# Layers 0 and 3 by image, and a recurrence that starts with one group of its input gates

## Chip, core and metric

One Trainium2 chip, one of its cores. The time is device time of one execution in microseconds; "before" is the median of three runs. Five engines work beside each other, each with an instruction queue of its own that it works off in order: TensorE (PE; its weight loads are shown as PEld), VectorE (DVE), ScalarE (ACT), GpSimd (POOL) and SyncE (SP), which here issues DMAs. All arithmetic is in float32.

## What is computed

Four layers on x of shape (4, 256, 32, 32): 4 images, 256 channels, 1024 tokens an image. The change touches layers 0 and 3; layer 1 (a rank-one attention with batch norm) and layer 2 (attention and a mixture of eight experts) stay.

```python
# layer 0: state-space block, then a gate per channel and image
u   = layernorm(tokens(x)) * norm_g + norm_b
y   = ssm(conv(in_proj(u))) * silu(z)
y   = y * rsqrt(mean(y * y, -1) + EPS) * rms_w
out = einsum('bld,ed->ble', y, out_w)
pooled = mean over tokens of out
attn   = sigmoid(relu(pooled @ se1_w.T + se1_b) @ se2_w.T + se2_b)
x   = x + out * attn
...
# layer 3: linear attention, then a recurrent cell over the tokens
f     = layernorm(t)
query = f @ W_qk[0] + b_qk[0];  key = f @ W_qk[1] + b_qk[1]
lam   = einsum('bnd,bne->bde', softmax(key, axis=1), f @ W_v + b_v)
bn    = batchnorm(lam) * gamma + beta          # over images and columns
t     = t + einsum('bnd,bde->bne', query, bn)
xi, xg, xo = (layernorm(t) @ U_k + b_k for k in 'ico')
for each of the 1024 tokens (all 4 images at once):
    i = sigmoid(xi_t + h @ V_i); g = tanh(xg_t + h @ V_c); o = sigmoid(xo_t + h @ V_o)
    c = h * c + i * g;  h = o * tanh(c)
t     = t + all h
```

The forget gate of the cell is computed in the reference but not used.

## The kernel before

The phases run one after another: set-up, layers 0 to 3. Instructions are written in source order; a scheduler in the framework then chooses their order on each engine by dependencies and estimated times, except where `_in_order` (L157) chains the instructions of a stretch of source on TensorE, VectorE and ScalarE so that each follows the one written before it. Tiles come from pools with a number of buffers; a tile waits until the buffer's last user is done, and a pool that opens on memory of a closed one waits for that one's users.

**Layer 0.** `_layer0` normalises and projects image by image and convolves. `_scan` (L376) goes over 8 chunks of 128 tokens, inside over the 4 images, 32 rounds: transposes and products on TensorE, an exp on ScalarE (L409), products with decays on VectorE and POOL, and at the end of a round the gated result in `zs` (L436). Then `_out_and_se` (L439) works over all images at once: 32 Squares on ScalarE with an accumulator (L449) give sums of squares per token; Sqrt and a reciprocal give rstd; then for each of 8 blocks of 512 tokens the rows are scaled (L459, VectorE), transposed (L463), evacuated with rms_w (L464), multiplied by out_w (L470), and evacuated by ScalarE with an accumulator that gives the sum over tokens (L473). After the last block come the mean, the two small products with Relu and Sigmoid (L478 to L491), and x is updated (L493). Layer 1's first products (L535) read x of all images.

**Layer 3, attention.** `_layer3_attention` (L1247) runs over images. Per image, two blocks of 512 tokens load two expert results each by SP's queue (L1282); POOL adds the two (L1285), VectorE adds them to x (L1287) and takes statistics (L1291, L1292). `_rsqrt` (L971) makes rstd for 8 columns by an integer start and four Newton steps of three VectorE operations. ScalarE normalises rows (L1302), TensorE turns them (L1268), VectorE copies them into `u` (L1273). Then key (L1318), its maximum, exp, transposed key times rows (L1343 to L1347), times W_v (L1357) give `lam` for the image; x is turned into `x_l` (ScalarE, L1271). After the images, `_batchnorm` on `lam` (L621 to L627, with a Sqrt), two passes for scale and shift (L1377, L1378), and the query weights are multiplied in once: `lam_q` (L1384) and `add_col` (L1394), so that later one product with `u` gives query times lam.

**Layer 3, recurrence.** `_layer3_lstm` (L1401) makes a few constants (L1429 to L1443). Tokens are in 8 groups of 128 steps. `ahead(n)` is a generator of parts for group n: `attended(n)` (attention output for these tokens, 16 parts of TensorE work and their adds, L1464 and L1458), then `input_gates(n)`: means (L1501), centring (L1487), squares, variance (L1511), Newton steps as "small" parts of one VectorE operation each, spread and p_r (L1545), and 64 parts for the gates, four for each of 16 sub-groups of eight steps (L1560, evacuated at L1571 into `xg`). Group 0's parts are run off before the first step. Each step then does: h times V (L1616, 48 products in three banks, TensorE), three transposes (L1645, VectorE), tanh and two sigmoids (L1646, ScalarE), the inputs of the next step from `xg` (L1607, TensorE), a scan for the cell (L1652), tanh (L1659), h (L1661) and the product for the next cell (L1663). One part of the next group's generator follows in each step; before the last step of a group all that are left are run off. `_in_order` fixes the order of all steps. POOL adds h to finished groups (L1585) and SP stores them.

Of the kernel before, what the change touches and what calls it, by code (L numbers as in the profile page):

```python
# [18 lines left out]
P = 128  # L19
# [47 lines left out]
NW = {"w_l0": 260 + 512 + 256 + 64, "w_l2": 768 + 8, "w_l3": 768, "w_u": 768, "w_v": 768}  # L67
# [91 lines left out]
def _in_order(s, start):  # L159


    engines = mybir.EngineType
    before = {}
    for i in s.nc.cur_bb.bb.instructions[start:]:
        if i.engine not in (engines.PE, engines.DVE, engines.Activation):
            continue
# [52 lines left out]
def _layer0(s):  # L219
# [6 lines left out]
    with ctx0 as ctx:  # L226
# [59 lines left out]
        _scan(s, xbc, zs, dt, decay, total, tail)  # L286
        _out_and_se(s, zs, w_out, w_se1, se2)
# [88 lines left out]
def _scan(s, xbc, zs, dt, decay, total, tail):  # L376
# [4 lines left out]
    with ExitStack() as ctx:  # L381
# [4 lines left out]
        for c in range(TPI):  # L386
            t = slice(off + c * P, off + (c + 1) * P)
            for b in range(B):
# [47 lines left out]
                nc.vector.tensor_mul(zs[:, n, :], zs[:, n, :], y.rearrange("p h d -> p (h d)"))  # L436


def _out_and_se(s, y, w_out, w_se1, se2):  # L439

    nc, tc = s.nc, s.tc
    with ExitStack() as ctx:
        keep = ctx.enter_context(tc.tile_pool(name="out_keep", bufs=1))
        pool = ctx.enter_context(tc.tile_pool(name="out", bufs=2))
        ps = ctx.enter_context(tc.tile_pool(name="out_ps", bufs=2, space=PSUM))
        ss = keep.tile([P, NT], F32, name="ss")
        for n in range(NT):
            sq = pool.tile([P, D], F32, name="sq")
            nc.scalar.activation(sq, y[:, n, :], AF.Square, accum_out=ss[:, n : n + 1])  # L449
        rstd = keep.tile([P, NT], F32, name="rstd")  # L450
        nc.scalar.activation(rstd, ss, AF.Sqrt, bias=s.eps, scale=1.0 / D)
        nc.vector.reciprocal(rstd, rstd)

        o = keep.tile([P, C, T], F32, name="o")
        part = keep.tile([P, C, NBLK], F32, name="part")
        for i in range(NBLK):
            yT = pool.tile([P, C, W], F32, name="yT")
            for n in range(i * TPB, (i + 1) * TPB):
                nc.vector.tensor_scalar_mul(y[:, n, :], y[:, n, :], rstd[:, n : n + 1])  # L459
            for k in range(C):  # L460
                pt = ps.tile([P, TPB, P], F32, name="pt")
                for j in range(TPB):
                    nc.tensor.transpose(pt[:, j, :], y[:, i * TPB + j, bass.ts(k, P)], s.ident)  # L463
                nc.vector.tensor_scalar_mul(  # L464
                    yT[:, k, :], pt.rearrange("p j q -> p (j q)"), s.col["rms_w"][:, k : k + 1]
                )
# [768 lines left out]
def _layer3(s):  # L1235
    with ExitStack() as ctx:
# [7 lines left out]
        _layer3_lstm(s, x, u, lam, add_col)  # L1244


def _layer3_attention(s, x, u, lam_q, add_col):  # L1247

# [513 lines left out]
```

## Time and profile before

| | us |
|---|---|
| median of three runs (3514.23 to 3514.61) | 3514.43 |
| profiled execution | 3514.67 |
| its span, first to last instruction | 3512.7 |
| TensorE busy | 3227.6 (92%) |
| VectorE busy | 2016.5 (57%) |
| ScalarE busy | 1245.0 (35%) |
| GpSimd busy | 416.3 (12%) |
| mean granted TensorE clock | 0.969 of full speed |

In the span, layer 0 ends and layer 1 begins near 359, the experts of layer 2 end near 1386, layer 3's first products with u start near 1426, step 1 of the recurrence at 1583, and the last h is there at 3506. A line of the timeline gives start and length in us, engine, line of the source, operation, output<-inputs and, in brackets, how long the engine sat idle before it and what ended that. A line of the windows gives the window and its length, then for PE, PEld, DVE, ACT and POOL the busy time and the number of instructions, then the granted clock of TensorE, the DMA engines' share and GB/s. "x16" counts instructions; a float32 product shows as two records. `x_l`, `u_l`, `w_l` are the names x_l3, u_l3 and w_l0, w_l2 or w_l3 with their numbers left out.

### The profile page before, as it was taken

The page shows a single profiled execution, that of the slowest core. Times are in us where ns is not written, and L with a number is a line of the kernel's source. Part 1 is how long each engine was busy: PE and PEld are TensorE (multiplying, and loading weights), DVE is VectorE, ACT ScalarE, POOL GpSimd, SP SyncE. Part 2 cuts the span into 40 slices and gives each one's busy share as a digit, 9 for nine tenths or more (in the row PEclk, how much of TensorE's full clock was granted, in tenths as well). Part 3 has the DMA queues.
Part 4 walks back from the last instruction along what each step waited for, and adds up shares of the span by engine and source line. Part 5 has one row for each costly group of instructions (what it writes and reads, how often), then busy time and mean ns, then how long its engine had stood idle before and what let it go on. Part 6 is the DMA issues. An engine that isn't in the chain of part 4 may idle for free.

```text
span 3512.7 us, 146893 instructions
## 1 busy us (share of the span) xinstructions
PE 3227.6 (92%) x65412; PEld 2536.4 (72%) x65412; DVE 2016.5 (57%) x8382; ACT 1245.0 (35%) x5047; POOL 416.3 (12%) x498
## 2 busy tenths in 40 slices
PE   7786899998999997789999999999999999999888
PEld 4464344447788886468888888888888888888776
DVE  5795534452211111747777776777777777767666
ACT  4623222223222222413334344343343343433333
POOL 0182001122433332100000000000000000000000
PEclk9898899999999999899999999999999999999999
DMA  1290001115556554100000000000000000000000
GB/s 67 80 303 5 9 0 37 37 50 197 195 189 219 208 190 165 60 2 4 4 11 4 5 10 4 4 10 4 6 9 5 10 4 5 10 4 5 10 4 10
DMA packets 79355, 189.31 MB, mean 54 GB/s; under 512 B 6592, under 2 KB 64256, under 8 KB 73728
## 3 DMA queue, kind: packets, MB, share of 16 engines
q0 software_dynamic: 16176, 116.06, 9.0%
q1 hardware_dynamic: 60624, 59.12, 5.7%
q8 instruction: 511, 8.37, 1.0%
q10 hardware_dynamic: 1920, 4.74, 0.4%
q14 instruction: 124, 1.02, 0.1%
HBM read 118.88 MB, written 61.02 MB: 51 GB/s over the span
## 4 chain that ended last, share of the span: by engine, by line
PE 41%; DVE 9%; ACT 4%; issue 2%; ACTq 0%; DVEq 0%
PE p_c L1616 11%; DVE turned L1645 7%; PE p_c L1607 7%; PE p_i L1607 4%; PE p_o L1607 4%; PE p_i L1616 4%; PE p_o L1616 4%; PE beside L1560 4%; ACT a_o L1646 2%; DVE x L1661 2%; ACT th L1659 2%; PE beside L1464 1%; PE beside L1501 0%; PE var L1511 0%; PE p_q L1384 0%
## 5 line engine op out<-in xcount | busy, mean ns | idle before, releaser
L1646 ACT ACTIVATE add<-turned 128x8 f32<-128x8 f32 x1024 | 214.3, 209 | 1027.5 <-DVE turned L1645 1027.5
L1616 PE MATMUL p_c<-w_v,x 128*4 128x64 f32 x16368 | 416.0, 219 | 72.8 <-DVE x L1661 71.0
L1607 PE MATMUL p_c<-xg,shift 128*128 128x64 f32 x2048 | 445.7, 299 | 0.0
L1616 PE MATMUL p_o<-w_v,x 128*4 128x64 f32 x16368 | 416.6, 219 | 0.1
L1616 PE MATMUL p_i<-w_v,x 128*4 128x64 f32 x16368 | 416.5, 219 | 0.0
L1607 PE MATMUL p_i<-xg,shift 128*128 128x64 f32 x2048 | 406.8, 280 | 0.0
L1645 DVE STREAM_TRANSPOSE turned<-p_c 128x64 f32<-128x64 f32 x1024 | 255.9, 250 | 257.1 <-PE p_c L1616 226.7
L1607 PE MATMUL p_o<-xg,shift 128*128 128x64 f32 x2048 | 396.0, 275 | 0.0
L1607 PEld LDWEIGHTS p_c<-xg,shift 128*128 128x128 f32 x2048 | 304.7, 188 | 117.6 <-issue 0.3
L1616 PEld LDWEIGHTS p_c<-w_v,x 128*4 128x4 f32 x16368 | 227.2, 85 | 196.3 <-DVE x L1661 121.2
L1661 DVE TENSOR_TENSOR x<-a_o,th 128x8 f32<-128x8 f32 x1024 | 171.9, 168 | 245.4 <-ACT th L1659 245.4
L1607 PEld LDWEIGHTS p_o<-xg,shift 128*128 128x128 f32 x2048 | 310.9, 192 | 0.3
L1607 PEld LDWEIGHTS p_i<-xg,shift 128*128 128x128 f32 x2048 | 304.8, 188 | 0.4 <-issue 0.3
L1187 PE MATMUL ph<-uT,w 128*128 128x256 f32 x1248 | 284.6, 386 | 20.8 <-DVE uT L1172 20.7
L1191 ACT ACTIVATE hT<-ph,w 128x256 f32<-128x256 f32 x312 | 147.9, 474 | 395.2 <-PE ph L1187 394.8
L1187 PEld LDWEIGHTS ph<-uT,w 128*128 128x128 f32 x1248 | 240.4, 194 | 58.2 <-DVE uT L1172 24.6
L1201 PE MATMUL po<-w,hT 128*128 128x256 f32 x1248 | 282.1, 379 | 0.0
L1616 PEld LDWEIGHTS p_o<-w_v,x 128*4 128x4 f32 x16368 | 281.2, 87 | 0.3 <-issue 0.3
L1616 PEld LDWEIGHTS p_i<-w_v,x 128*4 128x4 f32 x16368 | 281.2, 87 | 0.3
L1645 DVE STREAM_TRANSPOSE turned<-p_i 128x64 f32<-128x64 f32 x1024 | 271.6, 265 | 0.7 <-PE p_i L1607 0.3
L1645 DVE STREAM_TRANSPOSE turned<-p_o 128x64 f32<-128x64 f32 x1024 | 256.0, 250 | 0.3 <-PE p_o L1616 0.3
L1201 PEld LDWEIGHTS po<-w,hT 128*128 128x128 f32 x1248 | 234.0, 190 | 30.2
(437 smaller groups left out, 4395.4 us busy)
## 6 DMA issues: line engine op xcount, KB each, us to landing
sorted<-zeros SPq DMA_DIRECT2D x32, 1032.0 KB, 14.4
y_in<-results SPq DMA_DIRECT2D x16, 512.0 KB, 5.3
x<-in_x_dram SPq DMA_DIRECT2D x8, 512.0 KB, 8.7
tokens<-rows SPq DMA_DIRECT2D x4, 1024.0 KB, 4.7
x<-tokens SPq DMA_DIRECT2D x8, 512.0 KB, 4.2
out_dram<-x_l SPq DMA_DIRECT2D x64, 64.0 KB, 1.7
results<-y,place POOLq DMA_INDIRECT x78, 4.4
w_l<-in_w_l_dram ACTq DMA_DIRECT2D x1, 1092.0 KB, 11.4
```

Source lines behind the costliest of these rows:

```text
L1187: nc.tensor.matmul(ph, w1[:, k, bass.ts(n, P)], uT[:, k, :], start=k == 0, stop=k == C - 1,)
L1191: nc.scalar.activation(hT[:, n, :], ph, AF.Gelu, bias=b1[:, n : n + 1])
L1201: nc.tensor.matmul(po, hT[:, n, bass.ts(a, P)], w2[:, n, :], start=n == 0, stop=n == NHC - 1,)
L1464: nc.tensor.matmul(p, lam[:, k, b, bass.ts(m, P)], u_l3[:, k, b * L + n * SB : b * L + (n + 1) * SB], start=k == 0, stop=k == C - 1,)
L1560: nc.tensor.matmul(p[bass.ts(i, R), :], rows[:, k, bass.ts(g, R)], w_u[:, k, at : at + GQ // GC], start=k == 0, stop=k == C - 1, tile_posi ...
L1607: nc.tensor.matmul(p[:, :H], shift[:, row * B : row * B + P], xg[n][:, g, bass.ts(i, H)], start=True, stop=t == 0,)
L1616: nc.tensor.matmul(p[R * i : R * i + B, :H], hs[:, t - 1, bass.ts(k, B)], w_v[:, k, i * GQ + g * H : i * GQ + (g + 1) * H], start=False, s ...
L1645: nc.vector.transpose(zt.rearrange("p c w -> p (c w)"), pz[g][:, :H])
L1646: nc.scalar.activation(dst.rearrange("p (c b) -> p c b", c=C), zt[:, :, :B], f)
L1659: nc.scalar.activation(th, cell[:, :, 1], AF.Tanh)
L1661: nc.vector.tensor_mul(h, a_o, th)
```

## The change

Layer 0: the Squares move into the scan's rounds, one behind each `zs`; rstd comes from `_rsqrt`, once for chunks 0 to 6 and once for the last chunk; rms_w is multiplied into out_w once (`wo`); and the rest goes image by image, the mean taken of y before its projection (`mean`, `pooled`), the small products standing between the four projections of the image, in an order fixed on TensorE. Relu moves to VectorE. `_rsqrt` and the parts of the gates take three Newton steps instead of four, everywhere.

Layer 3: the constants are made and the bias is loaded ahead of the attention. VectorE adds both expert results to x; POOL's sum goes. Image 0's additions, statistics and normalisation stand in source order, in two halves; the other images' additions come behind image 0's last copy into `u`. `w_l3` holds the query weights in both layouts. The first 128 tokens' query of every image is computed outright (`q`), so that `attended(0)` uses `lam` and `q`; `lam_q` and `add_col` are made by a generator `queries`, whose eight parts are set between parts of group 0. A Sqrt on a spare value stands after the last image. Scale and shift of `lam` become one pass. Only the gates of the first sub-group are made before step 0; all further parts, of group 0 too, form one stream, one part a step, without the run-off at a group's end.

```diff
 def _scan(s, xbc, zs, ss, dt, decay, total, tail):
...
                 nc.vector.tensor_mul(zs[:, n, :], zs[:, n, :], y.rearrange("p h d -> p (h d)"))
+                sq = pool.tile([P, D], F32, name="sq")
+                nc.scalar.activation(sq, zs[:, n, :], AF.Square, accum_out=ss[:, c * B + b : c * B + b + 1])
...
 def _out_and_se(s, y, ss, w_out, w_se1, se2):
...
+        for t in (slice(0, NT - B), slice(NT - B, NT)):
+            nc.vector.tensor_scalar_mul(ms[:, t], ss[:, t], 1.0 / D)
+            for _ in _rsqrt(s, pool, rstd[:, t], ms[:, t]):
+                pass
+        for b in range(B):
...
+            for i in range(BPI):
+                for j in range(i * TPB, (i + 1) * TPB):
+                    n = b * TPI + j
+                    r = rstd[:, j * B + b : j * B + b + 1]
+                    if j % 2:
+                        nc.scalar.mul(y[:, n, :], y[:, n, :], r)
+                    else:
+                        nc.vector.tensor_scalar_mul(y[:, n, :], y[:, n, :], r)
...
+            start = len(nc.cur_bb.bb.instructions)
+            project(0, 0)
+            for m in range(C):
+                for k in range(C):
+                    nc.tensor.matmul(
+                        pooled[:, m : m + 1], wo[:, k, bass.ts(m, P)], mean[:, k : k + 1],
+                        start=k == 0, stop=k == C - 1,
+                    )
...
+            project(0, 1)
...
+            project(1, 0)
...
+            project(1, 1)
+            _in_order(s, start, (mybir.EngineType.PE,))
...
 def _layer3_attention(s, x, u, lam, q):
...
-                    nc.gpsimd.tensor_add(y[:, 0], y[:, 0], y[:, 1])
                     xr = s.xr[:, bass.ts(i, TPB), :]
-                    nc.vector.tensor_add(xr, xr, y[:, 0])
+                    for k in range(2):
+                        later(nc.vector.tensor_add(xr, xr, y[:, k]))
...
+                    if b == 0:
+                        normalise(g * TPB, TPB)
+                if b == 0:
+                    _in_order(s, start)
+                else:
+                    normalise(0, TPI)
...
+            nc.scalar.activation(pool.tile([P, C], F32, name="none"), total, AF.Sqrt)
...
 def _layer3_lstm(s, x, u_l3, lam, q, wq, constants):
...
-        for _ in ahead(0):
-            pass
-        start = len(nc.cur_bb.bb.instructions)
+        start = len(nc.cur_bb.bb.instructions)
+        fill = queries()
+        first = 2 * C * B + 1
+        smalls = 0
+        leading = ahead(0)
+
+        since = 0
+        for i, part in enumerate(leading):
+            smalls += bool(part)
+            since = 0 if part else since + 1
+            if smalls and since == GC * C:
+                break
+            if i in range(first + 1, first + 11, 2) or part and smalls % 4 == 1:
+                if next(fill, True) is None:
+                    end = len(nc.cur_bb.bb.instructions)
+        _in_order(s, start, (mybir.EngineType.PE,), end)
+        start = len(nc.cur_bb.bb.instructions)
+        parts = chain(leading, *(ahead(n) for n in range(1, L // SB)))
+        part = None
         inputs(0)
         for t in range(L):
-            n, i = divmod(t, SB)
-            if i == 0:
-                parts = ahead(n + 1) if (n + 1) * SB < L else iter(())
-                part = None
...
-            if i == SB - 1:
-                for _ in parts:
-                    pass
```

## The prediction, made before the changed kernel ran

> **What bounds the kernel now.** I read the page's chain first, then stage windows, then the timeline where a window shows an idle TensorE. The chain's shares cover only the time from 1516 us on and are split over the step loop:
>
> ```profile
> PE 41%; DVE 9%; ACT 4%; issue 2%; ACTq 0%; DVEq 0%
> ```
>
> The windows give the span by stage (length, then busy time and instruction count of each engine, then the granted clock):
>
> ```profile
> 295.00:311.00 16.00, 0.04 (x1) 0.07 (x1) 1.32 (x5) 14.47 (x66) 0.00 (x0) 0.50 0.00 1
> 311.00:359.00 48.00, 40.54 (x137) 21.16 (x138) 22.16 (x60) 13.08 (x36) 0.00 (x0) 0.93 0.00 0
> ...
> 1386.00:1423.00 37.00, 0.00 (x0) 0.00 (x0) 20.40 (x55) 0.62 (x2) 16.54 (x7) 0.53 0.77 249
> 1423.00:1529.00 106.00, 96.54 (x416) 64.71 (x416) 58.50 (x165) 44.48 (x80) 4.89 (x2) 0.95 0.05 17
> 1529.00:1583.00 54.00, 42.34 (x645) 31.81 (x649) 25.86 (x97) 9.08 (x17) 0.00 (x0) 0.84 0.01 3
> 1583.00:3507.00 1924.00, 1849.17 (x59281) 1577.82 (x59280) 1348.42 (x6603) 768.18 (x4120) 26.88 (x56) 1.00 0.02 6
> ```
>
> The reader should see that 1924 us are the recurrence, which the change hardly touches, and that three places hold removable time: 295 to 311 (TensorE idle, ScalarE squaring), 1386 to 1423 (TensorE idle), and 1529 to 1583 (work done ahead of the second step). The timeline at these places:
>
> ```profile
> 295.00 0.43 DVE L436 TENSOR_TENSOR zs<-zs,y 128x256 f32<-128x256 f32 x1
> 308.42 1.28 ACT L451 ACT_TABLE_LOAD   x1
> 310.96 2.02 PE L463 MATMUL pt<-ident,zs 128*128 128x128 f32 x8 [16.98 <-DVE zs L459]
> 358.90 13.79 PE L535 MATMUL p<-x,w 128*32 128x512 f32 x64 [1.03 <-DVE x L493]
> ...
> 1400.03 2.34 POOL L1285 TENSOR_TENSOR y_in<-y_in 128x1024 f32<-128x1024 f32 x1 [12.49 <-DMA y_in<-results]
> 1402.40 1.23 DVE L1287 TENSOR_TENSOR x<-x,y_in 128x1024 f32<-128x1024 f32 x1 [16.10 <-POOL y_in L1285]
> 1410.57 2.31 DVE L984 TENSOR_SCALAR rstd<-half 128x8 int32<-128x8 int32 x1
> 1423.03 2.17 PE L1268 MATMUL p_x<-ident,rows 128*128 128x128 f32 x8 [37.58 <-ACT rows L1302]
> ...
> 1530.48 1.28 ACT L625 ACT_TABLE_LOAD   x1 [14.57 <-issue]
> 1534.24 9.34 PE L1384 MATMUL p_q<-lam,w_l 128*128 128x512 f32 x16 [5.65 <-DVE lam L1378]
> 1543.43 3.63 PE L1394 MATMUL p_b<-cols,lam 128*128 128x1 f32 x32
> 1549.12 4.76 PE L1464 MATMUL beside<-u_l,lam_q 128*128 128x128 f32 x24 [1.06 <-DVE x_l L1458]
> 1570.93 0.15 DVE L1661 TENSOR_TENSOR x<-a_o,th 128x8 f32<-128x8 f32 x1
> 1573.25 9.34 PE L1560 MATMUL beside<-w_u,u 128*32 128x96 f32 x304
> 1582.94 0.41 PE L1616 MATMUL p_c<-w_v,x 128*4 128x64 f32 x16
> ```
>
> What matters: step 0 has its h at 1571.1, but step 1 (the first L1616) starts at 1582.94, behind 15 groups of gates that only later steps need.
>
> **Layer 0, 295.4 to 358.9 (63.5 us).** The 32 Squares with their accumulator reads (32 x 0.40 = 12.9 us back to back) move into the scan, on ScalarE, busy 28.3 of 100 us there. Each now waits for its chunk's zs, and behind it in ScalarE's queue stands a later chunk's exp (L409), for which VectorE and then TensorE wait. In the trace one zs ends at 224.73 and the next exp starts at 225.57; another ends at 229.00, exp at 229.51. A Square of 0.40 + 0.19 fits in the first gap and delays the second by about 0.1. So I cost it at 0, with 0 to 3 us as ends; the cover gone is the slower rival below. Sqrt and its load leave; rstd becomes 1 + 4 + 9 VectorE operations of 0.2 us (spacing of the L990 to L994 rows), once for chunks 0 to 6, able to run under the scan, and once for the last chunk; wo costs 2 x 0.35 (row L459). I let TensorE start at 298 (296.5 if all but the last chunk's part hides, 301 if nothing does).
>
> From there TensorE is the bound. Per image: 16 transposes 2 x 1.04 = 2.1; projection 2 x 3.67 = 7.3; the new pooled product 8 records x 0.14 (the single-column var rows, 0.5 to 0.6 for four) = 1.1; p1 and p2 0.36 + 0.38. Sum 11.3, four images 45.0, plus 2.0 for the first evacuation and mean. L535 can then start at 345.0, because the per-image attention of the last image runs under its own last projections: p2 stands ahead of project(1,1), 1.7 us. Its weights wait for the last p1, also before that. ScalarE (4 scalings 0.3, 4 evacuations 0.7, 2 sigmoids 0.35: 4.7) and VectorE (about 5) stay under 11.3. Gain 358.9 - 345.0 = **13.9** (5 with 2 us lost per image boundary and 3 in the scan; 17 at best).
>
> **Newton steps, 4 to 3.** 3 x 0.2 = 0.6 on the path in layer 0's first image (14.2 to 17.5) and in layer 1 (377 to 381.5): **1.2** (0 to 1.2). In layer 2 they are parts beside attention: 0, or 1 us either way, as the later parts shift against it.
>
> **Layer 3 to the first u.** The POOL sum of the two halves goes; VectorE adds both (2 x 1.22). POOL's reading of both halves and its 2.34 before the first x leave the chain, and so do three VectorE instructions of 2.2 to 2.3, normally 0.16, that stood beside POOL sums (one is in the rows above). Block 0 is there at 1400.0 (POOL's wait ended), block 1 at 1403.4. In order: first add before 1400.0, second to 1401.3, four statistics 1.85, rsqrt and shift 14 x 0.2 = 2.8: 1405.9. Block 1: 2.4 + 1.85 + 2.8: 1413.0; rows 2.1, transposes and two copies of u: about 1416.5, against 1430.95 now. Gain 14.5. The larger w_l3 (256 KB more) and the four b_l issues (1.76 on ScalarE's queue) come at 1386, where ScalarE is idle to 1422; w_v now lands about 1394.7, a later end by 1 us would still lie before the first block.
>
> The other images' adds now come after image 0's u, and cost VectorE 4.9 instead of 2.4 each: adds 4.9, statistics 3.7, rsqrt 2.8, u 2.7, top 2.4, kt 3.0, su and lam 1.8 make 21.3 of an image's 24.0 us. It fits, but not freely: the one image that now runs beside such preparation takes 26.1 (1430.95 to 1457.06) against 24.0. Giving back 2.1 for one to two more images, I take 2.5. The query product q (4 matmuls of 128x512, 8 x 0.43 = 3.4) lies in TensorE's idle 1528.6 to 1534.2; without that cover it costs 3.4. Net **12.0** (7 to 16).
>
> **From the last lam to step 1 (1530.5 to 1582.9).** Sqrt's load (1.28) moves under image 3. After the two scale activations four small operations of 0.2 and one 0.81 pass per half instead of two: lam at 1533.2. The p_q block (9.34) and p_b (3.63) leave the path, as do 1.7 us of constants: attended starts on lam and q at 1533, 32 records x 0.2: 1539.6. Then in TensorE's given order: four means 0.7 each, and five queries of 4 x 0.25 + 4 x 0.11 = 1.45 (rows L1347, L1394) under which VectorE centres: 4 x 2.15 + 1.45 = 10.0; var 16 x 0.15 = 2.3: 1552.0. Three more queries 4.35 against a VectorE chain of 3.0: 1556.3; p_r and rstd 0.7; two half groups of gates 0.55 + 0.55 + 0.3; the step's three inputs 0.9, transposes, the sigmoid load 1.28, step 0: h at about 1561.5, step 1 at 1561.7. Gain 1582.9 - 1561.7 = **21.2** (17 to 24: eight queries are 11.6 us, of which 4 would come back if centre and VectorE's chain overlapped less than assumed).
>
> **Steps.** 60 parts of group 0 join; a group has 116 parts instead of 119. 60 + 7 x 116 = 872 steps carry one, 833 now. A step with a part takes 1.88, one without 1.873: 39 x 0.007 = 0.3 us lost (0 to 6 if the moved parts meet POOL's adds). A group of gates takes four parts and serves eight steps, so none is awaited.
>
> **Sum.** -13.9 - 1.2 - 12.0 - 21.2 + 0.3 = -48.0. The profiled execution took 3514.67 (span 3512.7 and 1.97 around it), 0.24 above the median: 3514.43 - 48.0 = **3466.4**.
>
> Two rules, which the sum does not use. "ScalarE: Activation LUTs", What ACT_TABLE_LOAD costs, puts a drain of 1380 ns behind each 1283 ns load. Here the load at 1530.48 ends at 1531.76 and the activation starts at 1531.78, so no drain shows; with it the three loads taken off the path would be worth 4.1 us more, 3462.3. "TensorE: Matmul & The Clock Gate", What's actually happening, halves the clock after an idle window of some 3.4 us; the clock here is 0.56 to 0.58 in 1562 to 1570. If the new serial head let the array cool the same way, its 25 us of TensorE work would grow, by my estimate from that page 5 us at most: 3471.
>
> **Rivals.** (a) VectorE becomes the bound in attention: three images at 26.1 and a late u give 7 instead of 12, and image boundaries in layer 0 lose 2 us each with the scan 3 longer, 5 instead of 13.9: 3480. For it: 21.3 of 24.0 busy. Against: VectorE's waits there end on TensorE. (b) The head gains little, since queries stand ahead of the chain in TensorE's order (11.6 us exposed, none hidden): 21.2 - 11.6 = 9.6, 3478. Against: VectorE needs about 1.2 us per centre anyway. (c) The edit does not do what it says: the rest of group 0 drains before step 1, because the order leaves it ahead; 11.8 (1571.1 to 1582.9) stays, 3478. Against: the step order now contains the parts. (d) Slower: in the scan, each Square sits before the next chunk's exp and undoes the overlap. The chunk becomes exp 0.6, m_h 1.0, py 1.1, three VectorE operations 1.3, Square 0.6 and about eleven hops of 0.2 = 6.8 against 4.2 (134 us by 32): 2.6 x 32 = 83, 3549. It decides from 48 / 32 = 1.5 us a chunk. Against: the exp starts after the previous zs already and is done 1.75 us ahead of its use (230.11, used 231.86).
>
> **How the numbers follow.** Forecast 0.70 (3456 to 3476), (a) 0.11, (b) and (c) 0.12 together, (d) 0.04, no change 0.03. All best ends together give 58.2 (17 + 1.2 + 16 + 24) and one more in layer 2: 3455, the low end. All weak ends give 22 (5 + 0 + 7 + 17 less 6 in the steps, less 1), 3492; few will meet, and the range stops at 3484, beyond (a) to (c). A measurement of this kernel tells about 0.2% (7 us) from no change. Faster is everything but (d) and no change, less 0.01: 0.93; same 0.03; slower 0.04.
>
> **What would show it.** Layer 0: first L535 near 345 and Squares between L409s with the scan's end within 3 us of 295.4. Layer 3: no POOL sums, u complete some 30 us after the last scatter's issue instead of 44, image spacing 24 to 26. Head: first h-product about 31 us after the last lam statistics, not 52. Steps: 1.87 to 1.88 throughout. A scan longer by 10 us, or steps above 1.90, would make the prediction wrong.

## The result, and the profile after

| | before | after |
|---|---|---|
| median, us (four runs each) | 3514.33 | 3461.33 |
| lowest to highest | 3510.33 to 3514.61 | 3459.89 to 3467.84 |
| profiled execution, and its span | 3514.67, 3512.7 | 3467.84, 3465.9 |
| mean granted TensorE clock | 0.969 | 0.974 |

The ratio is 0.9855, with a 95% interval of 0.9838 to 0.9872: 53.0 us less by the medians. The forecast was 3466.4, within 3456 to 3476, so the median lies 5.1 us below it. The two profiled executions differ by 46.8. The profiled one is the slowest of the changed kernel's four, so the stages below are compared within this pair of profiles, and what varies between executions is taken up with the experiments.

The windows of the changed kernel, cut near the ends of the same stages (not at exactly the same events as the windows of before; the table further down is cut by events):

```profile
293.00:297.00 4.00, 0.00 (x0) 0.00 (x0) 3.28 (x25) 0.84 (x3) 0.00 (x0) 0.50 0.00 2
297.00:344.00 47.00, 46.83 (x196) 26.93 (x200) 18.57 (x64) 18.74 (x57) 0.00 (x0) 0.94 0.02 3
344.00:351.00 7.00, 7.00 (x65) 2.22 (x58) 3.94 (x11) 1.38 (x2) 0.00 (x0) 1.00 0.25 97
1364.00:1395.00 31.00, 8.39 (x21) 3.80 (x22) 16.43 (x58) 4.84 (x9) 0.59 (x1) 0.56 0.78 261
1395.00:1503.00 108.00, 95.57 (x401) 63.06 (x401) 66.89 (x182) 42.54 (x76) 0.00 (x0) 0.95 0.09 30
1503.00:1533.40 30.40, 27.95 (x194) 23.21 (x193) 11.84 (x53) 9.76 (x29) 0.00 (x0) 0.89 0.00 1
1533.40:3460.00 1926.60, 1864.54 (x59746) 1590.35 (x59746) 1353.72 (x6612) 768.13 (x4120) 26.88 (x56) 1.00 0.02 6
```

Behind the scan TensorE waits 5.60 us where it waited 16.98, and is then busy for 46.83 of 47 us up to layer 1. The window around the expert results, which ends with the first complete u, is 31 us long. In the last 30.40 us of the head, the stretch from the last lam to step 1, TensorE is busy for 27.95. The recurrence keeps its length to within 3 us.

Each event's time, read from the timeline, gives the difference of the two profiles stage by stage:

| stage | before | after | difference | forecast |
|---|---|---|---|---|
| start to the end of the scan (last zs) | 295.43 | 293.29 | -2.1 | -0.6 |
| scan's end to layer 1's first products | 63.47 | 50.37 | -13.1 | -13.9 |
| these 64 products (L535, now L578) | 13.79 | 7.07 | -6.7 | 0 |
| rest of layer 1 and layer 2, to the first y_in load | 1021.05 | 1018.51 | -2.5 | -0.6 |
| first y_in load to u of image 0 | 37.21 | 26.00 | -11.2 | -14.5 |
| u of image 0 to lam of image 3 | 98.17 | 105.96 | +7.8 | +2.5 |
| last lam to step 1 | 53.82 | 32.20 | -21.6 | -21.2 |
| step 1 to the last h | 1922.90 | 1925.67 | +2.8 | +0.3 |
| sum | | | -46.6 | -48.0 |

The remaining 0.2 is rounding and what follows the last h. That the sum of the forecast is so close is partly luck, because its misses cancel: 6.7 us were gained where nothing was forecast, and 3.4 more than forecast in the scan and in layer 2, which vary by as much between executions; the way to the first u gained 3.3 less, the attention gave back 5.3 more, and the steps lost 2.5 more.

Layer 0 in the timeline after:

```profile
292.87 0.42 DVE L440 TENSOR_TENSOR zs<-zs,y 128x256 f32<-128x256 f32 x1
296.67 1.71 ACT L477 ACTIVATE zs<-zs,rstd 128x256 f32<-128x256 f32 x4 [2.77 <-DVE rstd L1037]
297.17 1.09 PE L483 MATMUL pt<-ident,zs 128*128 128x128 f32 x4 [5.60 <-ACT zs L477]
342.20 2.73 DVE L537 SCALAR_TENSOR_TENSOR x<-po,att,x 128x512 f32<-128x512 f32 x4
343.66 7.07 PE L578 MATMUL p<-x,w 128*32 128x512 f32 x64
```

The line of the products now has no wait in brackets: by 343.66 only the last image's update is still running. Before the change all eight updates of 128x1024 began at the end of the layer:

```profile
357.47 9.66 DVE L493 SCALAR_TENSOR_TENSOR x<-o,att,x 128x1024 f32<-128x1024 f32 x8 [0.71 <-ACT att L491]
```

Each took 1.21 us, the products need them one after another, and the first products had run at a granted clock of 0.50 (359 to 362) and 0.57 (362 to 365). That is where the 6.7 us were, in the waits and the low clock together.

### The profile page after: what moved, and what is told of

The parts are those of the page before. It is cut to its first block, busy times and chain, and to the rows that moved or that the text cites. A ratio compares the mean times of both kernels' runs of the same rounds, so it can differ in the third digit from the quotient of the medians.

```text
span 3465.9 us, 147036 instructions
## 1 busy us (share of the span) xinstructions
PE 3237.8 (93%) x65492; PEld 2546.7 (73%) x65492; DVE 1998.7 (58%) x8361; ACT 1253.7 (36%) x5081; POOL 399.1 (12%) x490
## 4 chain that ended last, share of the span: by engine, by line
PE 46%; DVE 9%; ACT 4%; issue 2%; DMA 0%; ACTq 0%; SPq 0%; DVEq 0%
PE p_c L1721 11%; PE p_c L1712 8%; DVE turned L1762 6%; PE p_i L1712 5%; PE p_i L1721 5%; PE p_o L1721 5%; PE p_o L1712 5%; PE beside L1662 4%; ACT a_o L1763 2%; DVE x L1775 2%; ACT th L1773 1%; PE beside L1569 1%; PE p_u L1441 1%; PE p_mm L1412 1%; PE beside L1602 1%
## 6 DMA issues: line engine op xcount, KB each, us to landing
w_l<-in_w_l_dram ACTq DMA_DIRECT2D x1, 1092.0 KB, 11.4
```

## Experiments

Each kernel is the changed kernel with the edit shown, run beside the kernel before on the same chip; ratios are to that. The changed kernel's own spread matters for all of them, so it came first.

### The changed kernel again

> The changed kernel once more, unchanged. The three executions of it without a profile took 3459.9 to 3461.5, the profiled one 3467.8. Expected: the timed runs at 3460 to 3462. If a new profile comes out near 3461, comparing its stages with the first profile names the stage that lost 6.5 us there; if the loss is spread evenly over the steps it is the profile or the clock, if it stands in one place (the attention of layer 3, or the first steps) it is a state that this place can fall into.

Measured: 3470.64 (3464.79 to 3472.90), ratio 0.9860 (0.9844 to 0.9877), on a chip where the kernel before took 3517.80. The expected 3460 to 3462 did not come back; the ratio did. Over the eleven profiles of this study in which layer 2 and the scan are those of the changed kernel, three places vary: the end of the scan (291.4 to 294.9), the time from layer 1's products to the first y_in load (1018.0 to 1026.5, and 1021.1 before), and the low clock in the head. So a difference of less than some 5 us between two executions says nothing, and the verdicts below rest on stages of the profiles first. Why layer 2 varies by 8 us was not followed, and which of the three made the first profiled execution 6.5 us longer than its neighbours stays open.

### Layer 0's part undone

```diff
-        ss = keep.tile([P, NT], F32, name="ss")
-        _scan(s, xbc, zs, ss, dt, decay, total, tail)
-        _out_and_se(s, zs, ss, w_out, w_se1, se2)
+        _scan(s, xbc, zs, dt, decay, total, tail)
+        _out_and_se(s, zs, w_out, w_se1, se2)
```

(both functions as before the change)

> Layer 0's part of the change undone (the Squares after the scan, the root on ScalarE, o and part for all tokens, one pair of SE products at the end), all the rest as changed, three Newton steps kept. Theory A, that layer 1's first products (64 records, 13.8 us before and 7.1 after) went faster because every x update stands ready when they begin: they go back to 13 to 14 us, and the kernel is slower than the changed one by 13 (the stage itself) plus 6.7, near 3481. Theory B, that their faster pace came from something else (the clock of that moment, three Newton steps): they stay near 7 and the kernel is slower by 13 only, near 3474.

Measured: 3492.09, ratio 0.9922 (0.9906 to 0.9939), 21.5 above the changed kernel on the same chip. The products' line in its timeline:

```profile
355.94 13.79 PE L537 MATMUL p<-x,w 128*32 128x512 f32 x64 [0.83 <-DVE x L495]
```

The 13.79 us are back with three Newton steps and everything behind unchanged, and the wait for the updates with them. From the scan's end to the end of these products it takes 76.8 us, against 56.9 in the changed kernel's profile on the same chip: 19.8 us, of which 13.1 is the stage forecast and 6.7 the products. Theory A holds: the products are slow again when the updates come late. How much of the 6.7 belongs to the waits and how much to the low clock (0.50 and 0.66 in the first 6 us here) was not separated. This run also tests the Squares by themselves: with them behind the scan again, the scan ends at 293.0, within the 291.4 to 294.9 seen with them in it.

### Additions held by the last u copy of the image before

```diff
-                if b == 0:
-                    ahead = done
+                ahead = done
```

> In layer 3's attention the additions of every image wait for the last u copy of the image before it, where the changed kernel makes all later images wait for image 0's alone. Theory A, that image 1's first key came 31.6 us after image 0's u (26.1 before) because four additions and eight statistics of image 2 stand among image 1's Newton steps on VectorE: 26 to 28 us, and 3 to 5 us less than the changed kernel. Theory B, that the period comes from elsewhere (the shared landing of the y_in and weight loads, TensorE's low clock at the first p_u products): the period stays above 30 and the time within 1 us. Theory C: the additions now come too late for the next image, and each later period grows by 2 us or more: slower by 4 or more.

Measured: 3465.00 (3460.59 to 3477.23), ratio 0.9859 (0.9838 to 0.9881): by time not distinguishable. By stage, from image 0's u to image 1's it takes 29.5 us (35.3 and 35.0 in the two profiles of the changed kernel), then 24.8 and 27.0 (23.5 and 19.8, 24.4 and 19.8); from image 0's u to the last lam 104.3 (106.0 and 108.1). So theory A is right about the place, and a part of theory C's loss follows. The u of image 3 comes late because its four additions now stand behind image 2's last copy, but the head waits for lam: from one image's last lam to the next it takes 24.8, 26.2 and 25.0 us for images 1 to 3 (30.4, 24.2 and 23.7, and 31.7, 24.2 and 25.1, in the changed kernel). Image 1 gains 5.6 to 6.8, image 2 loses 2.0, and 1.7 to 3.9 remain to the last lam. These are the rows of VectorE in the changed kernel that make image 1 late:

```profile
1395.15 2.35 DVE L1386 TENSOR_TENSOR x<-x,y_in 128x1024 f32<-128x1024 f32 x2
1403.38 1.19 DVE L1386 TENSOR_TENSOR x<-x,y_in 128x1024 f32<-128x1024 f32 x1
1413.87 1.19 DVE L1386 TENSOR_TENSOR x<-x,y_in 128x1024 f32<-128x1024 f32 x1
1416.20 0.15 DVE L1020 TENSOR_SCALAR v<-mv 128x8 f32<-128x8 f32 x1
1416.94 0.42 DVE L1390 BATCH_NORM_STATS2 stats<-x 128x6 f32<-128x256 f32 x1
1422.85 0.15 DVE L1367 SCALAR_TENSOR_TENSOR shift<-mv,rstd 128x8 f32<-128x8 f32 x1
```

The additions from 1403.38 to 1413.87 and the statistics beside the Newton steps (1416.20 on) are image 2's. Image 1's shift begins 27.6 us after image 0's u.

### All gates of group 0 ahead of the first step

```diff
-            if smalls and since == GC * C:
-                break
...
-        parts = chain(leading, *(ahead(n) for n in range(1, L // SB)))
...
+            n, i = divmod(t, SB)
+            if i == 0:
+                parts = ahead(n + 1) if (n + 1) * SB < L else iter(())
+                part = None
```

> All input gates of group 0 stand ahead of the first step again, and the parts of group n+1 begin with group n's first step, as before the change; queries, q and the rest as changed. Theory A, the forecast's: the gates of group 0 that were moved beside the steps were worth about 12 us, so near 3473 against the changed kernel's 3461, and the steps after the start take 1.87 at once instead of 2.5, 3.2 and 2.7, because the array is warm from the gates. Theory B: the moved gates only lengthen the first steps by what they save: within 2 us of the changed kernel.

Measured: 3484.18, ratio 0.9896 (0.9880 to 0.9913), 13.5 above the changed kernel on the same chip. From the last lam to the second h it takes 45.3 us, against 32.5; the steps then take 1.88 at once. Theory A holds: the moved gates are worth what the forecast's third rival priced them at (11.8). The edit also brings back the run-off at each group's end, but that is not in the price: from the second h to the last it takes 1921.7 us, against 1924.0 and 1923.4.

### Queries ahead

```diff
         fill = queries()
+        for _ in fill:
+            pass
...
-            if i in range(first + 1, first + 11, 2) or part and smalls % 4 == 1:
-                if next(fill, True) is None:
-                    end = len(nc.cur_bb.bb.instructions)
+            end = len(nc.cur_bb.bb.instructions)
```

> The eight query pairs (the product lam by wq and its column, with their copies) all stand ahead of the first attended products on TensorE, where the changed kernel fills them in among group 0's means, variances and Newton steps. Theory A, the forecast's: they were hidden in waits of TensorE, and ahead they cost what their matmuls last, 8 pairs of 1.1 us at the full clock and up to 2 at the low one: the stretch from the last lam to the first h grows by 9 to 12 us. Theory B, that the head is bound by TensorE throughout (it is busy in nearly every record from the last lam on), so that it does not matter where they stand: within 2 us of the changed kernel.

Measured: 3470.94, ratio 0.9869 (0.9850 to 0.9889). From the last lam to the second h 35.5 us, against 32.5 and 33.9 in the changed kernel's two profiles: 1.6 to 3.0 more, a part of it from a clock that stayed at 0.50 to 0.55 over the Newton steps. Not 9 to 12: theory A is out. TensorE now waits for 3.4 us in all over means, variance and Newton steps (0.16, 0.38, 2.14 and 0.73 idle in four windows of 3 us), and these waits are what the queries had filled.

### GpSimd's sum for images 1 to 3

```diff
-                    for k in range(2):
-                        later(nc.vector.tensor_add(xr, xr, y[:, k]))
+                    if b == 0:
+                        for k in range(2):
+                            nc.vector.tensor_add(xr, xr, y[:, k])
+                    else:
+                        nc.gpsimd.tensor_add(y[:, 0], y[:, 0], y[:, 1])
+                        later(nc.vector.tensor_add(xr, xr, y[:, 0]))
```

> For images 1 to 3 of layer 3's attention GpSimd sums the two halves of y_in again and VectorE adds once, as before; image 0 as changed; the additions still wait for image 0's last u copy. Theory A, that VectorE's load made image 1 late (four additions of 1.2 us more for images 1 and 2 ahead of image 1's Newton steps): image 1's period falls from 31 or 32 toward 28, time 2 to 4 us less than the changed kernel. Theory B, that the order alone does it, image 2's statistics standing ahead of image 1's Newton steps whatever the additions cost: the period falls by the additions removed there alone, under 2 us, time the same within noise. Against both: GpSimd's sum (2.1 to 2.5 us each) comes late and the period grows.

Measured: 3470.89, ratio 0.9872 (0.9853 to 0.9890). From image 0's u to image 1's 32.7 us, to the last lam 104.6. Halving the additions helps image 1 by 2.3 to 2.6, ordering them by 5.5 to 5.7. In the time neither shows. These stages begin at image 0's u, which itself came later here: 27.7 us after the first y_in load, against 26.0 and 26.3 in the changed kernel's two profiles (rows that show why stand with the second of the three versions below).

### Four Newton steps

```diff
-    for _ in range(3):
+    for _ in range(4):
```

(in `_rsqrt` alone)

> Four Newton steps instead of three in the helper that all layers but the input gates use; nothing else is changed. In the kernel before the last product of layer 0's scan ended at 295.4, in nine profiles with three steps at 292.1 to 293.7. Theory A, that the fourth step held up layer 0's front and that layer 2's length does not feel it (from layer 1's first products to the first y_in it took 1018 to 1027 in ten profiles, and 1021 before): the scan ends near 295, the time is 2 to 4 us above the changed kernel. Theory B, that the front's 2 to 3 us came from elsewhere: the scan ends near 292.5, and the time is within 1 us. Theory C: the step costs in layer 2's 32 groups too, and its length grows beyond 1027.

Measured: 3480.81 (3473.62 to 3485.76), ratio 0.9895 (0.9878 to 0.9912): 12 to 14 us worse than the changed kernel by the ratios, and not where any of the three theories put it. The scan ends at 294.1, within the spread with three steps; layer 2 takes 1022.3, likewise. The time is lost in layer 3, from the first key to the last lam (117.7 us against 110.8 and 112.8) and from there to the second h (36.3 against 32.5 and 33.9). Rows of its VectorE and TensorE:

```profile
1401.12 2.35 DVE L1386 TENSOR_TENSOR x<-x,y_in 128x1024 f32<-128x1024 f32 x2
1421.59 0.15 DVE L1020 TENSOR_SCALAR v<-mv 128x8 f32<-128x8 f32 x1
1431.03 0.16 DVE L1367 SCALAR_TENSOR_TENSOR shift<-mv,rstd 128x8 f32<-128x8 f32 x1
...
1531.82 2.26 PE L1612 MATMUL var<-avg,sq 128*128 128x1 f32 x16
1533.94 2.05 PE L1537 MATMUL beside<-lam,w_l 128*128 128x256 f32 x4
```

Image 1's Newton steps last from 1421.6 to 1431.0 where they lasted from 1416.2 to 1422.9, because the longer chain lets more of image 2's work and image 0's end in between. And the queries behind the variance run at 2.05 us, at half the clock, which stayed at 0.50 to 0.54 for 24 us here (1533 to 1557). A step counted at 0.2 us an operation is therefore no measure of what it costs in this order. The attention accounts for 4.9 to 6.9 of the loss; the rest stands in the head and the first steps, and one profile does not show whether the fourth step made the low clock last longer there.

### The variance products 64 columns wide

```diff
-            var = ps.tile([P, TT], F32, name="var")
+            V = 64 if n == 0 else 1
+            var = ps.tile([P, TT, V], F32, name="var")
...
-                        var[:, i : i + 1], sq[:, k, bass.ts(i, P)], s.avg[:, :1],
+                        var[:, i, :], sq[:, k, bass.ts(i, P)], s.avg[:, :V],
...
-            nc.vector.tensor_scalar_add(v, var, EPS)
+            nc.vector.tensor_scalar_add(v, var[:, :, 0], EPS)
```

> The variance products of group 0 stream 64 columns instead of 1 (all columns of that matrix are equal, column 0 is used); nothing else is changed. In three profiles of kernels with this head the granted clock fell to 0.50 for 3 to 8 us right after these one-column products, while TensorE was busy in 3.00 of 3.00 us by its records, and again over steps 1 to 3. Theory A, that the gate counts columns streamed, so that this stretch of one-column products reads as idle: the clock stays at 1.00 from 1510 to step 1, the head is 2 to 4 us shorter. Theory B, that the gate answers to the real gaps (1.1 us idle of 3 at the first Squares, 1.2 us at the table loads): the low stretch stays, the time is the same within noise or 0.5 us more.

Measured: 3465.07, ratio 0.9857 (0.9838 to 0.9875). The head in the changed kernel, first TensorE's rows, then windows, in which the third number from the end is the granted clock:

```profile
1519.55 1.93 PE L1612 MATMUL var<-avg,sq 128*128 128x1 f32 x16
1521.33 2.01 PE L1537 MATMUL beside<-lam,w_l 128*128 128x256 f32 x4
```

```profile
1519.00:1522.00 3.00, 3.00 (x24) 2.89 (x23) 0.35 (x3) 0.43 (x2) 0.00 (x0) 0.90 0.02 5
1522.00:1525.00 3.00, 3.00 (x11) 2.55 (x10) 1.84 (x12) 0.43 (x2) 0.00 (x0) 0.50 0.00 0
1537.00:1540.00 3.00, 3.00 (x63) 2.66 (x63) 1.07 (x6) 0.48 (x3) 0.00 (x0) 0.50 0.04 8
```

and with 64 columns:

```profile
1522.50 1.98 PE L1613 MATMUL var<-avg,sq 128*128 128x64 f32 x16
1524.31 1.08 PE L1537 MATMUL beside<-lam,w_l 128*128 128x256 f32 x4
```

```profile
1523.00:1526.00 3.00, 3.00 (x24) 2.87 (x23) 1.21 (x8) 0.34 (x3) 0.00 (x0) 1.00 0.00 0
1526.00:1529.00 3.00, 3.00 (x41) 2.76 (x43) 1.17 (x8) 1.23 (x7) 0.00 (x0) 1.00 0.00 0
1535.00:1538.00 3.00, 3.00 (x114) 2.59 (x107) 2.21 (x12) 1.13 (x6) 0.00 (x0) 1.00 0.03 8
```

Sixty-four columns cost the sixteen products 0.05 us together, and the query behind them takes 1.08 instead of 2.01. The second h comes 30.5 us after the last lam (32.4 to 33.9 in the four profiles with the changed kernel's head and the low clock), and from the second h to the fifth it takes 1.87 each (2.49, 3.24 and 2.71 in the changed kernel's first profile). What theory A forecast came, and theory B is out, since TensorE still waits 1.05 us for lam and 1.23 us at the table loads here and the clock stayed at 1.00; that the gate counts columns is the reading that fits. In the profiles of the changed kernel and its versions the clock fell behind the one-column products in eight of nine, and behind those with 64 columns in none of four. The ninth is the version with every addition held; its second h comes 30.5 us after the last lam as well, which confirms the price by another way.

### Three versions meant to beat both, and a control

The three versions have the 64 columns and this line, which loads the steps' function table behind the last scaling of lam:

```diff
+        nc.scalar.activation(
+            keep.tile([P, 1], F32, name="none"), lam[:, C - 1, B - 1, D - 1 :], AF.Sigmoid
+        )
```

They differ in what holds the additions: image 0's u for image 1 and image 1's u for images 2 and 3; the last u of each image for the next one, with GpSimd's sum; and, third, the shift of each image for the next one:

```diff
                 else:
-                    normalise(0, TPI)
+                    ahead = normalise(0, TPI)
```

(`normalise` returns the shift's instruction; image 1 still waits for image 0's u)

> A version meant to beat both: image 1's additions wait for image 0's u, those of images 2 and 3 for image 1's u; group 0's variance products stream 64 columns; and a spare Sigmoid right behind the last scaling of lam loads the function table that the steps use, so that no table is loaded between the queries and step 0. Expected: the attention from first key to last lam 108 instead of 110 to 112, the head 1.3 us less for the table that was loaded with nothing beside it and 2 to 4 less for the clock: 4 to 8 us below the changed kernel. If the held additions only move the wait to a later image (26.3 for the last period where image 2 holds image 3) the first is worth 0 to 1; if the clock does not answer to the columns, 1 to 3 in all.

Measured: 3461.34 (3459.85 to 3462.31), ratio 0.9842 (0.9824 to 0.9859), 4.6 to 6.3 us below the changed kernel by the ratios, with overlapping intervals. First key to last lam takes 109.6, not 108. From image 0's u 28.2, 28.6 and 22.9 us to the next ones; to the last lam 104.7, so the hold moved the wait from image 1 to image 2. The table's part is as expected. In the changed kernel ScalarE loads two tables behind the last query, and TensorE then waits 1.23 us for step 0's h; in this one it loads one, early, and none later:

```profile
1529.23 1.28 ACT L1763 ACT_TABLE_LOAD   x1
1531.23 1.28 ACT L1763 ACT_TABLE_LOAD   x1
```

```profile
1509.93 1.28 ACT L1735 ACT_TABLE_LOAD   x1 [0.79 <-DVE lam L1487]
```

The second h comes 29.2 us after the last lam, 1.3 less than with the 64 columns alone.

> A version meant to beat both: the additions of each image wait for the last u copy of the image before it; GpSimd sums the two halves of y_in for images 1 to 3, so that only two additions wait and not four; group 0's variance products stream 64 columns; the spare Sigmoid behind the last scaling of lam. Expected: the period from image 0's u to image 1's 28 to 30 (35 in the changed kernel), that of image 2 to 3 24 to 25 instead of the 27.0 seen with four additions held; from image 0's u to the last lam 101 to 103 (105 to 108); head 28 to 29; time 3456 to 3460, 8 to 12 below the changed kernel on the same chip. Rival: TensorE's 24 us an image bound these periods anyway, the stretch stays at 104, and the time equals that of the version before it, 3461.

Measured: 3467.50, ratio 0.9857 (0.9841 to 0.9873). The attention missed its 101 to 103: 31.2, 27.4 and 24.7 us from u to u, 108.5 to the last lam. Two things went against it. Image 1's shift is early (15.6 us after image 0's u) but its first u copy begins only 7.2 us after that: ScalarE normalises the rows from 1417.83 to 1421.87, and TensorE then takes image 1's transposes a few at a time (from 1421.46 and from 1424.19) between image 0's products of kt and rows, 1.99 us each. And image 0's u came 30.3 us after the first y_in load (27.7 and 27.9 in the two other versions with GpSimd's sum, 25.7 to 26.9 in the nine profiles with three Newton steps and without it). GpSimd's sums for image 1 begin at 1385.55 and 1388.44, and beside them VectorE's shift takes 2.34 us (0.16 in the changed kernel) and two additions 4.51 (2.48):

```profile
1385.57 2.34 DVE L1367 SCALAR_TENSOR_TENSOR shift<-mv,rstd 128x4 f32<-128x4 f32 x1
1387.83 4.51 DVE L1387 TENSOR_TENSOR x<-x,y_in 128x1024 f32<-128x1024 f32 x2
```

The head is as short as in the version before it, 29.3.

The control is this second version with one column:

> The same version with one column in group 0's variance products, as in the changed kernel. If the clock answers to the columns streamed, its profile shows the granted clock at 0.5 to 0.9 right after the variance products and over steps 1 to 3, and the time is 3 to 5 us more, in most of its executions (5 of 6 profiles with one column had it, none of 2 with 64). If the 64 columns did nothing, the two agree within 1.5 us and their profiles are alike.

Measured: 3470.09, ratio 0.9874 (0.9858 to 0.9891). The clock fell to 0.50 behind the variance again, though not over the steps, and the head is 32.6 against 29.3: 3.3 us between two kernels that differ in the columns alone. Their times differ by 2.6, with overlapping intervals. The windows behind the variance, with one column and with 64:

```profile
1529.00:1532.00 3.00, 3.00 (x13) 2.64 (x11) 0.81 (x5) 0.43 (x2) 0.00 (x0) 0.50 0.00 0
```

```profile
1532.00:1535.00 3.00, 3.00 (x27) 2.77 (x30) 1.33 (x9) 1.13 (x5) 0.00 (x0) 1.00 0.00 0
```

The low stretch over the steps is thus absent both with 64 columns and the late table loads, and here with one column and the table loaded early; what starts that second stretch is not shown.

> A version meant to beat both: image 1's additions wait for image 0's last u copy, those of images 2 and 3 for the shift of the image before (the last of its Newton steps on VectorE), some 7 us earlier than its last u copy; 64 columns in group 0's variance products; the spare Sigmoid. Theory A, that the order on VectorE alone made image 1 late and that the wait for the last u copy made images 2 and 3 late where it was tried: from image 0's u to image 1's 28 to 30 us, then 24 to 25 for each of the others, from image 0's u to the last lam 100 to 103 (105 to 108 in the changed kernel, 104 to 105 with additions held by the last u copy), 3457 to 3461 on a chip where the changed kernel takes 3461 to 3470. Theory B, that what image 1 gains is lost again by images 2 and 3 whatever holds their additions: 104 to 105 once more, and 3461 to 3465. The clock is expected at 1.00 from the variance products to step 3 in both.

Measured: 3454.26 (3452.42 to 3456.30) beside 3510.61, ratio 0.9839 (0.9826 to 0.9853). From image 0's u to the last lam 102.5, within theory A, though not by its parts: u to u it takes 24.8 for image 1 (28 to 30 expected), 24.3 for image 2 and 28.3 for image 3 (24 to 25 expected for both). The clock is at 1.00 from the variance on and the head 29.2. VectorE's rows:

```profile
1407.98 0.17 DVE L1020 TENSOR_SCALAR v<-mv 128x8 f32<-128x8 f32 x1
1411.95 0.17 DVE L1367 SCALAR_TENSOR_TENSOR shift<-mv,rstd 128x8 f32<-128x8 f32 x1
1412.03 2.35 DVE L1387 TENSOR_TENSOR x<-x,y_in 128x1024 f32<-128x1024 f32 x2
```

Image 2's first additions begin 0.08 us after the start of image 1's shift, which stands 17.6 us after image 0's u instead of 27.6. This is the best kernel of the study: 56.4 us below the kernel before in its runs, where the changed kernel gained 53.0 and 47.2 in its two. The intervals of the ratios overlap, so that it beats the changed kernel is likely and not settled.

## Why the forecast held, point by point

The total came out nearer than its parts, which partly cancel. By two of its own signs the forecast missed: images followed each other in attention at up to 35 us instead of 24 to 26, and three steps took more than 1.90 us.

**Bound.** The three places named held the time, and the recurrence was not touched by much. **Squares in the scan** at nothing: right. In both profiles the scan ended at most 3 us away from 295.4 (293.3 and 292.4), it ends no earlier with the Squares taken out of it, and rival (d) with its 83 us did not occur. **Layer 0's stage:** 13.1 against 13.9, each image behind the first taking about 11.0 us instead of 11.3, no loss at the image boundaries; undone, it comes back. **What stood ahead of layer 1** was the term left out: the forecast ended the stage at the first L535 and carried its 13.79 over unchanged, although the row shown for it names the wait for x L493, and the change replaces eight late updates by updates per image. It was worth 6.7.

**Newton steps** at 1.2: their places in the forecast (layer 0's front, layer 1) show nothing beyond the spread. Undoing them costs 12 to 14, most of it in layer 3, a place the forecast did not count at all: about half in the order of the attention, another part where the clock is low. That is the price of putting the step back into the changed kernel; what its removal alone would have done to the kernel before was not tried.

**Layer 3 to the first u:** right in mechanism, 11.2 instead of 14.5. The steps that were mis-sized are seen in these rows:

```profile
1374.88 1.23 DVE L1386 TENSOR_TENSOR x<-x,y_in 128x1024 f32<-128x1024 f32 x1 [9.86 <-DMA y_in<-results]
1376.93 1.22 DVE L1386 TENSOR_TENSOR x<-x,y_in 128x1024 f32<-128x1024 f32 x1 [0.83 <-DMA y_in<-results]
1382.98 2.48 DVE L1386 TENSOR_TENSOR x<-x,y_in 128x1024 f32<-128x1024 f32 x2
1385.83 0.67 DVE L1341 COPY u_l<-p_x 128x512 f32<-128x512 f32 x1
```

The second half is awaited for another 0.83 us, so block 0's additions end 8.9 us after the first load and not 7.6; and block 0's u copies (two of 0.67) stand between block 1's statistics, in VectorE's fixed order, so that block 1 takes 8.3 us to its shift and not 7.1. Transposes and copies at the end took some 0.5 more than the 3.5 forecast.

**Given back in the attention:** the sentence "It fits, but not freely" was right and the 2.5 us behind it wrong. Up to the last lam layer 3 gained 3.4 us in all (11.2 less 7.8; 1.0 in the second profile), where the forecast had 12.0 with 7 as its low end. The count of busy time (21.3 of 24.0 us) says nothing about order: image 2's additions came ahead of image 1's Newton steps on VectorE, and image 1's u came 35 us after image 0's instead of 27. From image 0's u on, the last lam of each image follows after 27.7, 30.4, 24.2 and 23.7 us, against 26.7, 24.3, 23.5 and 23.7 before, so that 6.1 of the 7.8 stand at image 1. This is the mechanism of rival (a), which put it at 5 more than the forecast; it was 5.3 more. That the order causes it is shown by the held versions: image 1's lam follows after some 24.8 us both where all additions wait for the last u copy and where they wait for the shift.

**Head:** 21.6 against 21.2, and here too two misses cancel. With 64 columns, at the full clock, the stage takes 28.9 us, a gain of 24.9 and above the upper end of 24; the forecast's own terms make it 32.6 (1529.1 to 1561.7). The largest of them that is too long is attended, 32 products at 0.2 us: the row that it was priced from, at 1549.12, ran at a granted clock of 0.65, and now 30 of them take 4.18 us:

```profile
1506.10 4.18 PE L1569 MATMUL beside<-q,lam 128*128 128x128 f32 x30 [1.04 <-DVE lam L1487]
```

The low clock, which the sum did not have, took 3.3 of this back in the first profile. Rival (c) is excluded and its price confirmed (11.4 to 12.8 by stages). Rival (b) was over-priced: queries ahead cost 1.6 to 3.0, not 11.6, since TensorE has only 3.4 us of waits for them to fill. The table that the steps' Sigmoid loads costs 1.3, as counted.

**Steps:** 1.87 to 1.88, but for the three intervals from the second h to the fifth, which account for the 2.8 (8.43 instead of 5.61). The forecast's two sentences on rules of the Trainium skill: a cooled array was real. It gave 5 us at most as an estimate for it; measured are 3.3 up to the second h and 2.8 in the steps behind it in the changed kernel's first profile, 2.0 and 1.2 in its second. The drain did not show here either: the load at 1531.23 ends at 1532.51, and ScalarE's next operation starts at 1532.52.

## What to carry to other kernels

A total that comes out right does not confirm its terms: compare stage by stage, and hold each term against the spread of its stage between executions. A stage's end is not its last instruction but the moment its consumer runs at full speed: read the row of the next stage's first instruction and its wait, and put what it waits for into the sum. Busy time that fits into a period does not show that the work fits: on an engine that executes in order, list what will stand ahead of the chain that the next stage waits for, and fix that order by the last instruction of that chain rather than by something later. Streams of one-column products count as work in the records but left the array at half clock behind them here; where a serial head stands ahead of a long loop, look at the granted clock in windows of 3 us.

## What the runs showed of the hardware

TensorE's granted clock fell to about half (0.50 to 0.56 in most of the windows of 3 us) right behind sixteen one-column products in eight of nine profiles, in seven of them though TensorE was busy for 3.00 of 3.00 us by its records; with 64 columns, as long in time (1.98 us against 1.93), it did not in any of four. "TensorE: Matmul & The Clock Gate", What's actually happening, in the Trainium skill has the clock depend on how busy the array has been in a free-running window of some 3.4 us. That the same kernel lost from the second h on in one profile (2.49, 3.24, 2.71) and from the first on in the other (2.16, 3.05), and one kernel with one column not at all, agrees with a window whose phase is not the kernel's; no run shows the window itself.

One table load of 1.28 us served both the Tanh and the Sigmoid of all steps when Sigmoid was asked for first, in four profiles; asked for in the other order, a load stood ahead of the first of each.

VectorE's operations took longer while GpSimd summed y_in: 2.34 us for a shift of 128x4 that takes 0.16 without it, 4.51 for two additions that take 2.48.
